# First attention: near distances as products over all features, far distances as products over 64 features a side in two halves of the rows

## Chip, core and metric

The kernel runs on one core of a Trainium2 chip. The metric is the device time of one execution in microseconds (us). TensorE (PE) multiplies, with its weight loads shown apart (PEld); VectorE (DVE), ScalarE (ACT) and GpSimd (POOL) work on rows; SyncE (SP) only issues DMAs. Each engine works through its own queue in order.

## The reference, cut to what matters

The network is an attention with relative positions, a mixture of experts, a second attention and the same mixture again, each added to its input. Only the first attention is changed. It has 4 batch rows of 1024 positions, 128 features, 8 heads:

```python
attn = einsum('bnqd,bnkd->bnqk', Q + rel_embed_bias, K)
positions = get_positional_embed(L, 192)      # (2 L - 1) x 192
rel_k = (positions @ w_rel_pos_k)             # for every distance and head
attn_pos = relative_shift(einsum('bnqd,nkd->bnqk', Q + rel_pos_bias, rel_k))
out = softmax(attn + attn_pos) @ V
```

The 192 features of a distance d are three kinds of 32 and the same 96 times the sign of d: exponentials of |d|, steps (1 where 2^n - 1 > |d|, for n = 1 to 32) and gamma densities of |d|. So on one side (d below 0, or d above 0) a sign is constant, and a step feature is constant between 2^n - 1 and the next power: from |d| = 127 to 1023 only the four steps n = 7 to 10 ever change.

## The kernel before

Work goes by blocks, one for each batch row and head (32 blocks), and each block by eight tiles of 128 query rows. Before the blocks, a setup loop over the heads turns and joins the weights (`turn_weights`, `join_weights`) and `distances` (L535) makes `relk`, the products of all 2048 distances' features with the head's joined weights: 128 x 2048 a head, kept in SBUF.

One loop over steps t (L706) writes out the order of the work by hand; its instructions stand on each engine in the order of the program:

- `relative(t + 5)` (L584): for tile i, the products of its 128 rows with a window of 1152 columns of `relk` (L594, 1024 columns into one PSUM buffer `rp`; L598, 128 columns into `rt`). ACT copies both into `xr` (L599, L600), and SP writes `xr` into a scratch tensor in DRAM (L603).
- `shift(t + 4)` (L606): SP reads the scratch back with rows one element shorter than they were written, which shifts each row by its number; this is `s`.
- `softmax(t)` (L614): content scores `sp` on PE (L622, 1024 columns), then one DVE instruction adds `s` and gives the row maximum (L627), then ACT takes the exponential and the row sum (L632).
- `transposed(t - 1)` (L635): DVE turns the probabilities in 32 x 32 squares into `at` (L641), and a reciprocal of the sum (L644).
- `values(m)` (L646), at the second step of the next block: 128 products of four row groups of 32 rows each (L655) into two PSUM buffers `op`; copies by ACT (L665) and DVE (L667) give `oT`. As `at` has one buffer, the first two tiles of a block are turned behind it, at its third step.
- `outputs` (L670), twice a block: four products `yp` (L674) and four DVE updates of the residual rows (L680).
- `make_keys` (L572), once a block: `kp` on PE (L576), copied by ACT to `kT` (L581).

PSUM has two pools here: `big` (three buffers of 1024 columns, for `rp`, `sp`, `op`, `kp`, taken in turn) and `small` (two buffers of 512 columns, for `rt`, `yp` and small products, taken in turn). They fill PSUM. A buffer is taken again when its last reader is done.

For three of the batch rows the routing of the experts (`dispatch`), and for each next batch row its layer norm (`rows`), run beside this loop in small steps.

One float32 product in the code is two records of PE in the trace.

Of the kernel before, what the change touches and what calls it, by code (L numbers as in the profile page):

```python
# [12 lines left out]
F32 = mybir.dt.float32  # L13
I32 = mybir.dt.int32
AF = mybir.ActivationFunctionType
ALU = mybir.AluOpType
AX = mybir.AxisListType

P = 128
B, L, D = 4, 1024, 128  # L20
NB = L // P
H = 8
R = 192
RW = 2 * L
WIN = L + P
E = 8
HID = 256
# [37 lines left out]
def block_kernel(ctx: ExitStack, tc: tile.TileContext, a: dict, out: bass.AP):  # L65
# [318 lines left out]
    with ExitStack() as sa:  # L384
# [6 lines left out]
        dram = sa.enter_context(  # L391
            tc.tile_pool(name="a_skew", bufs=8, space=bass.MemoryType.DRAM)
        )
        relk = [w1[:, :RW], w1[:, RW:], ring.rearrange("p a t d -> p (a t d)")]
        relk += [wp.tile([P, RW], F32, tag=f"relk{h}", name=f"relk{h}") for h in range(3, H)]

        joint = [wp.tile([P, 2, P], F32, tag=f"joint{h}", name=f"joint{h}") for h in range(H)]
        bo = wp.tile([P, D], F32, tag="a_bo", name="a_bo")
# [28 lines left out]
        with ExitStack() as s0:  # L427
# [39 lines left out]
            wr_views = (a["w_rel"][:R2, :], a["w_rel"][R2:, :])  # L467
            eb = wload("eb", [P, H], a["eb"], nc.gpsimd)
            rb = wload("rb", [P, H], a["rb"], nc.gpsimd)
            posf = {}  # L470
            for k in range(3):
                wq.load("wq", P, a["w_qs"], nc.sync, k)
                other = nc.scalar if k == 0 else nc.sync
                wk.load("wk", P, a["w_ks"], other, k)
                wr0.load("wr0", R2, wr_views[0], nc.sync, k)
                wr1.load("wr1", R2, wr_views[1], other, k)
                wv.load("wv", P, a["w_vs"], nc.sync, k)
                load_wo(other, k)
                if k == 0:
                    for c in (0, 2):  # L480
                        for half, eng in ((0, nc.sync), (1, nc.scalar if c == 0 else nc.sync)):
                            posf[half, c] = wload(
                                f"pos{half}_{c}", [R2, L],
                                a["pos"][half * R2 : (half + 1) * R2, c * 512 : (c + 2) * 512], eng,
                            )
            for b in range(B):
                nc.sync.dma_start(out=xs[b], in_=x_view[b])
                if b == 0:
                    nc.sync.dma_start(out=bo, in_=a["b_out"].to_broadcast([P, D]))
            turns, halves, scores = {}, {}, {}  # L490

            def turn_weights(h):
# [25 lines left out]
            def join_weights(h):  # L518
                wT, qe, qr, kk = turns.pop(h)
                jp = small(f"jp{h}")  # L520
                nc.tensor.matmul(jp[:, :P], kk, qe, start=True, stop=True)
                nc.tensor.matmul(
                    jp[:, P : 2 * P], wT[:, 2 * P : 3 * P], wo[h], start=True, stop=True
                )
                for k in range(2):
                    nc.tensor.matmul(
                        jp[:R2, (2 + k) * P : (3 + k) * P],
                        wT[:, 3 * P + k * R2 : 3 * P + (k + 1) * R2], qr, start=True, stop=True,
                    )
                nn = w0.tile([R2, 2 * P], F32, tag="nn", name=f"nn{h}", bufs=2)  # L530
                nc.scalar.copy(nn, jp[:R2, 2 * P :])
                nc.vector.tensor_copy(joint[h].rearrange("p k c -> p (k c)"), jp[:, : 2 * P])
                halves[h] = nn

            def distances(h, c):  # L535
                nn = halves[h]
                ps = big(f"rkps{h}_{c}")
                for half in range(2):
                    for k in range(2):
                        nc.tensor.matmul(  # L540
                            ps[:, k, :], nn[:, half * P : (half + 1) * P],
                            posf[half, c][:, k * 512 : (k + 1) * 512],
                            start=(half == 0), stop=(half == 1),
                        )
                out_rk = relk[h][:, c * 512 : (c + 2) * 512]
                if c == 0:
                    nc.scalar.copy(out_rk, ps.rearrange("p a c -> p (a c)"))
                else:
                    nc.vector.tensor_copy(out_rk, ps.rearrange("p a c -> p (a c)"))

            xn_a0 = w0.tile([P, NB, D], F32, tag="xn", name="xn_a0")
            first_rows = rows(0, xn_a0)
            with tc.manual_schedule():
                turn_weights(0)
                turn_weights(1)
                join_weights(0)
                for h in range(H):
                    distances(h, 0)
                    if h + 1 < H:
                        join_weights(h + 1)  # L560
                    distances(h, 2)
                    if h + 2 < H:
                        turn_weights(h + 2)
                    if 2 <= h <= 4:
                        next(first_rows, None)

        hp = sa.enter_context(tc.tile_pool(name="a_h", bufs=2))
        N = len(blocks) * NB
        AHEAD = 5
        keys, written, skewed, probs, rinvs, sums, turned_sums = {}, {}, {}, {}, {}, {}, {}  # L570

        def make_keys(m):  # L572
            b, h = blocks[m]
# [7 lines left out]
            nc.scalar.copy(kT, kp.rearrange("p a c -> p (a c)"))  # L581
            keys[m] = kT

        def relative(n):  # L584

            b, h = blocks[n // NB]
            i = n % NB
            rk = relk[h]
            lhsT = xTs[b][:, i * P : (i + 1) * P]
            base = (NB - 1 - i) * P  # L590
            xr = hp.tile([P, WIN], F32, tag="xr", name=f"xr{n}", bufs=3)
            rp = big(f"rp{n}")
            for c in range(2):
                nc.tensor.matmul(  # L594
                    rp[:, c, :], lhsT, rk[:, base + c * 512 : base + (c + 1) * 512], start=True, stop=True
                )
            tail = small(f"rt{n}")
            nc.tensor.matmul(tail[:, :P], lhsT, rk[:, base + L : base + WIN], start=True, stop=True)  # L598
            nc.scalar.copy(xr[:, :L], rp.rearrange("p a c -> p (a c)"))  # L599
            nc.scalar.copy(xr[:, L:WIN], tail[:, :P])  # L600

            scratch = dram.tile([P, WIN + 1], F32, tag="skew", name=f"skew{n}")
            nc.sync.dma_start(out=scratch[:, :WIN], in_=xr)  # L603
            written[n] = scratch

        def shift(n):  # L606

            scratch = written.pop(n)
            s = hp.tile([P, L], F32, tag="s", name=f"s{n}", bufs=7)
            shifted = bass.AP(scratch.tensor, scratch.offset + P, [[WIN, P], [1, L]])  # L610
            nc.sync.dma_start(out=s, in_=shifted)
            skewed[n] = s

        def softmax(n):  # L614

            b, h = blocks[n // NB]
            i = n % NB
            kT = keys[n // NB]
            s = skewed.pop(n)
            sp = big(f"sp{n}")  # L620
            for c in range(2):
                nc.tensor.matmul(  # L622
                    sp[:, c, :], xTs[b][:, i * P : (i + 1) * P], kT[:, c * 512 : (c + 1) * 512],
                    start=True, stop=True,
                )
            nmax = hp.tile([P, 1], F32, tag="nmax", name=f"nmax{n}", bufs=4)
            nc.vector.tensor_tensor_reduce(  # L627
                out=s, in0=sp.rearrange("p a c -> p (a c)"), in1=s, scale=-1.0, scalar=BIG,
                op0=ALU.add, op1=ALU.min, accum_out=nmax,
            )  # L630
            total = hp.tile([P, 1], F32, tag="total", name=f"total{n}", bufs=6)
            nc.scalar.activation(s, s, AF.Exp, bias=nmax, scale=-1.0, accum_out=total)  # L632
            probs[n] = (s, total)
# [36 lines left out]
        def outputs(m, oT, i0):  # L670
            b, h = blocks[m]
            yp = small(f"yp{m}_{i0}")
            for k in range(4):
                nc.tensor.matmul(  # L674
                    yp[:, k * P : (k + 1) * P], oT[:, i0 + k, :, :].rearrange("p g c -> p (g c)"),
                    joint[h][:, 1, :], start=True, stop=True,
                )
            for k in range(4):
                x_t = xs[b][:, i0 + k, :]
                nc.vector.scalar_tensor_tensor(  # L680
                    x_t, yp[:, k * P : (k + 1) * P], rinvs[m][:, i0 + k : i0 + k + 1], x_t,
                    ALU.mult, ALU.add,
                )
# [19 lines left out]
        coming = iter(())  # L703
        oT = None
        with tc.manual_schedule():
            for t in range(-AHEAD, N + 5):  # L706
                m, i = divmod(t - NB, NB)
                if t == -AHEAD:
                    make_keys(0)
                if 0 <= t + AHEAD < N:  # L710
                    relative(t + AHEAD)
                if 0 <= t + AHEAD - 1 < N:
                    shift(t + AHEAD - 1)
                if t == 4:
                    for w_t, view in late:
                        nc.gpsimd.dma_start(out=w_t, in_=view)
# [28 lines left out]
                    transposed(t - 1)  # L745
                if 1 <= m <= 3 and i in (2, 4, 6):
                    experts_weights(3 * (m - 1) + i // 2 - 1)
                if m >= 0 and i == 2:
                    outputs(m, oT, 0)
                if m >= 0 and i == 4:  # L750
                    outputs(m, oT, 4)
                    if m % H == H - 3:
                        next(coming, None)
# [540 lines left out]
```

## Time and profile before

| what | value |
|---|---|
| median of 23 runs | 2745.55 us |
| lowest and highest | 2740.62, 2756.26 us |
| the profiled execution: time | 2753.86 us |
| its span, first to last instruction | 2751.8 us |
| mean granted TensorE clock | 0.974 |
| first `values` starts | 136.4 us into the span |
| first attention ends (last `yp`) | 1615 us |
| one block of the first attention | 47.09 us, 24 of 31 of them within 1 us |

Durations below come from the one profiled execution, which was 8.3 us (0.3%) longer than the median. A duration in the trace is one instruction's record. ACT and DVE records overlap the next one's by up to 0.1 us, and PE's records include the time until a result has left the array, so that what an instruction holds its engine for is read from start to start. Idle time of an engine matters only where it is on the path that ends last.

### The profile page before, as it was taken

The page shows a single profiled execution, that of the slowest core. Times are in us where ns is not written, and L with a number is a line of the kernel's source. Part 1 is how long each engine was busy: PE and PEld are TensorE (multiplying, and loading weights), DVE is VectorE, ACT ScalarE, POOL GpSimd, SP SyncE. Part 2 cuts the span into 40 slices and gives each one's busy share as a digit, 9 for nine tenths or more (in the row PEclk, how much of TensorE's full clock was granted, in tenths as well). Part 3 has the DMA queues.
Part 4 walks back from the last instruction along what each step waited for, and adds up shares of the span by engine and source line. Part 5 has one row for each costly group of instructions (what it writes and reads, how often), then busy time and mean ns, then how long its engine had stood idle before and what let it go on. Part 6 is the DMA issues. An engine that isn't in the chain of part 4 may idle for free.

```text
span 2751.8 us, 47428 instructions
## 1 busy us (share of the span) xinstructions
PE 2675.0 (97%) x18928; PEld 1637.0 (59%) x18928; DVE 1407.1 (51%) x3278; ACT 1334.1 (48%) x2478; POOL 536.9 (20%) x691
## 2 busy tenths in 40 slices
PE   8999999999999999999999999999999999999895
PEld 4465656566565666666665666655555455554563
DVE  3345353545545454545445355466546466574454
ACT  2434353444444443544534345555566656556442
POOL 3121000000200001200002005543212215122275
PEclk9999999999999999999999999989999999999897
DMA  8777565755757565666657413300000001000143
GB/s 217 234 225 244 164 220 172 231 190 170 232 168 228 179 199 189 208 199 204 228 182 231 164 54 108 87 14 7 1 1 1 1 1 32 1 7 11 57 128 100
DMA packets 150955, 363.59 MB, mean 132 GB/s; under 512 B 16384, under 2 KB 74272, under 8 KB 150608
## 3 DMA queue, kind: packets, MB, share of 16 engines
q1 hardware_dynamic: 134832, 319.89, 36.0%
q0 software_dynamic: 15264, 39.92, 5.7%
q8 instruction: 150, 2.46, 0.4%
q10 hardware_dynamic: 640, 0.75, 0.1%
q14 instruction: 69, 0.57, 0.1%
HBM read 176.69 MB, written 183.76 MB: 131 GB/s over the span
## 4 chain that ended last, share of the span: by engine, by line
PE 92%; DVE 3%; DMA 2%; POOL 1%; issue 1%; ACT 1%; SPq 0%; ACTq 0%; POOLq 0%; DVEq 0%
PE op L655 16%; PE rp L594 16%; PE sp L622 15%; PE t_b L1079 9%; PE s_b L1022 9%; PE o_b L1100 5%; PE h_f L830 3%; PE h_g L830 3%; PE yp L674 2%; PE rt L598 2%; PE kp L576 2%; PE rkps L540 2%; PE yp_f L859 1%; PE qk_b L969 1%; PE yp_g L859 1%
## 5 line engine op out<-in xcount | busy, mean ns | idle before, releaser
L627 DVE CUSTOM_DVE_ANT_0 s<-sp,s 128x1024 f32<-128x1024 f32 x256 | 313.0, 1223 | 373.5 <-PE sp L622 373.2
L632 ACT ACTIVATE s<-s,nmax 128x1024 f32<-128x1024 f32 x256 | 294.1, 1149 | 413.9 <-DVE nmax L627 413.9
L622 PE MATMUL sp<-kT,xT 128*128 128x512 f32 x1024 | 484.4, 596 | 2.3 <-ACT kT L581 1.6
L655 PE MATMUL op<-at,xrep 32*128 32x256 f32 (+1 forms) x8448 | 455.8, 371 | 3.4 <-DVE nmax L627 3.1
L655 PEld LDWEIGHTS op<-at,xrep 32*128 32x128 f32 x8448 | 423.9, 187 | 47.0 <-issue 23.5
L1079 PE MATMUL t_b<-qm,ka_b 32*128 32x512 f32 x1152 | 424.4, 665 | 3.4 <-DVE m L1031 1.4
L1082 ACT ACTIVATE pt_b<-t_b 128x512 f32<-128x512 f32 x576 | 333.0, 615 | 160.0 <-PE t_b L1079 127.8
L1022 PE MATMUL s_b<-ka_b,qa_b 32*128 32x128 f32 (+3 forms) x2304 | 384.2, 408 | 1.6 <-DVE m L1031 1.3
L1031 DVE TENSOR_REDUCE m<-s_b 128x1 f32<-128x512 f32 (+3 forms) x480 | 287.1, 649 | 112.2 <-PE s_b L1022 87.4
L641 DVE STREAM_TRANSPOSE at<-s 128x1024 f32<-128x1024 f32 x256 | 315.8, 1238 | 0.2 <-ACT s L632 0.2
L594 PE MATMUL rp<-relk,xT 128*128 128x512 f32 x640 | 303.0, 596 | 0.0
L1022 PEld LDWEIGHTS s_b<-ka_b,qa_b 32*128 32x128 f32 x2304 | 227.1, 195 | 107.7 <-issue 41.7
L599 ACT COPY xr<-rp 128x1024 f32<-128x1024 f32 x256 | 256.3, 1001 | 71.0 <-issue 36.5
L622 PEld LDWEIGHTS sp<-kT,xT 128*128 128x128 f32 x1024 | 175.1, 191 | 128.0 <-issue 123.3
L667 DVE COPY oT<-op 128x256 f32<-128x256 f32 (+1 forms) x66 | 24.4, 411 | 398.7 <-PE op L655 398.7
L594 PEld LDWEIGHTS rp<-relk,xT 128*128 128x128 f32 x640 | 116.4, 190 | 127.1 <-issue 124.7
L665 ACT COPY oT<-op 128x256 f32<-128x256 f32 (+1 forms) x66 | 20.9, 369 | 351.9 <-PE op L655 351.9
L1079 PEld LDWEIGHTS t_b<-qm,ka_b 32*128 32x128 f32 x1152 | 149.0, 189 | 59.5 <-DVE m L1031 24.6
L170 POOL COPY beats<-beats 1x1 f32<-1x1 f32 x240 | 42.9, 179 | 602.5 <-DVE beats L167 601.7
L1100 PE MATMUL o_b<-pt_b,va_b 128*32 128x512 f32 x1152 | 146.2, 628 | 0.0
L594 PE MATMUL rp<-w,xT 128*128 128x512 f32 x256 | 121.2, 596 | 0.2 <-ACT xr L599 0.2
L598 PEld LDWEIGHTS rt<-relk,xT 128*128 128x128 f32 x320 | 60.8, 190 | 76.5 <-issue 75.3
(274 smaller groups left out, 3087.9 us busy)
## 6 DMA issues: line engine op xcount, KB each, us to landing
skew<-xr SPq DMA_DIRECT2D x256, 576.0 KB, 3.9
s<-skew SPq DMA_DIRECT2D x256, 512.0 KB, 4.5
ring<-sorted SPq DMA_DIRECT2D x40, 256.0 KB, 3.3
xrep<-stored POOLq DMA_DIRECT2D x16, 512.0 KB, 8.5
sorted<-joint POOLq DMA_DIRECT2D x4, 1472.0 KB, 18.4
res_f<-y_f SPq DMA_DIRECT2D x20, 256.0 KB, 2.5
res_g<-y_g SPq DMA_DIRECT2D x20, 256.0 KB, 2.4
w<-in_w POOLq DMA_DIRECT2D x16, 256.0 KB, 5.5
```

Of the source, the lines that this page charges most:

```text
L594: nc.tensor.matmul(rp[:, c, :], lhsT, rk[:, base + c * 512 : base + (c + 1) * 512], start=True, stop=True)
L599: nc.scalar.copy(xr[:, :L], rp.rearrange("p a c -> p (a c)"))
L622: nc.tensor.matmul(sp[:, c, :], xTs[b][:, i * P : (i + 1) * P], kT[:, c * 512 : (c + 1) * 512], start=True, stop=True,)
L627: nc.vector.tensor_tensor_reduce(out=s, in0=sp.rearrange("p a c -> p (a c)"), in1=s, scale=-1.0, scalar=BIG, op0=ALU.add, op1=ALU.min, acc ...
L632: nc.scalar.activation(s, s, AF.Exp, bias=nmax, scale=-1.0, accum_out=total)
L641: nc.vector.transpose(sums[m][:, i, :], s)
L655: nc.tensor.matmul(ops[g // 2][:, g % 2, :n], xrep[r, j, :], at[r, tiles, j * 32 : (j + 1) * 32], start=(j == 0), stop=(j == 31),)
L1022: nc.tensor.matmul(banks[m][:, q * w : (q + 1) * w], qa[r, k + q, tok], ka[r, k0 : k0 + w], start=True, stop=True,)
L1031: nc.vector.tensor_reduce(m2[:, 4 * g + k : 4 * g + k + nh, c], ps[:, : nh * w].rearrange("p (k c) -> p k c", c=w), AX.X, ALU.max,)
L1079: nc.tensor.matmul(ps, ka[rows[g], j * P : (j + 1) * P], qm[rows[g], :], start=True, stop=True)
L1082: nc.scalar.activation(pt[:, g, :], ps, AF.Exp, scale=HD ** -0.5)
L1100: nc.tensor.matmul(op[g * 32 : (g + 1) * 32, :], va[:, j, :], pt[:, g, :], start=(j == i), stop=(i == 0 or j == i - 1),)
```

## The change

The window of 1152 distances of a tile is cut in three. The 256 nearest are products over all 192 features, as before, from a table `near` of 256 columns a head (instead of 2048). For the distances from 128 on, on either side, the step features are taken out, and what is left are 64 features a side (32 exponentials, 32 gamma densities):

- `distances` makes, for every head, `near` (256 columns), eight columns of sums of step weights (`sums_of`, four ranges on each side), and `sides`, 128 x 128: joined weights of the 64 features of the negative side and of the positive one.
- `make_sides(m)`, once a block: `qf` = the rows' coefficients for those features, 128 x 1024, side 0 in partitions 0 to 63 and side 1 in 64 to 127.
- `relative` now works on a pair of tiles, at every second step, six tiles ahead. Two products of 264 columns (`near` and the eight sums), and the far distances of both tiles, whose two sides are products of 64 rows each, side 0 from one half of the partitions and side 1 from the other, into two `big` buffers, `far` 0 and `far` 1.
- DVE copies the eight sums into `xr`, ACT copies the 256 near columns, and ACT writes the far ones in pieces between the limits 127, 255, 511 and 1023, each with its sum of steps as a bias.
- The tiles of a block go in the order 0, 7, 1, 6, 2, 5, 3, 4, so that a pair has 896 far columns on each side. `shift` reads both tiles of a pair; `outputs` stands at steps 3 and 5 instead of 2 and 4 of a block; `s` has 9 buffers instead of 7, `xr` 4 instead of 3.
- In the setup only 256 columns of all the features and 896 of the far ones are loaded for each side, and the first batch row is loaded before the last weights.

```diff
+RANGES = ((7, 127), (8, 255), (9, 511), (10, 1023))
+NEAR = 2 * P
+FAR = L - P
...
-            def distances(h, c):
-                nn = halves[h]
-                ps = big(f"rkps{h}_{c}")
+            def distances(h):
+                nn, wT, qr = halves.pop(h)
+                ps = big(f"rkps{h}")
                 for half in range(2):
...
+                    nc.tensor.matmul(
+                        ps[:, 0, :NEAR], nn[:, half * P : (half + 1) * P], nearf[half],
+                        start=(half == 0), stop=(half == 1),
+                    )
+                nc.tensor.matmul(ps[:, 1, :R], qr, wT[:, 3 * P :], start=True, stop=True)
+                nT = w0.tile([P, R], F32, tag="nT", name=f"nT{h}", bufs=2)
+                nc.scalar.copy(nT, ps[:, 1, :R])
+                nc.scalar.copy(near[h][:, :NEAR], ps[:, 0, :NEAR])
...
+                for k, op in ((0, ALU.subtract), (1, ALU.add)):
+                    nc.vector.tensor_tensor(
+                        side[:, k, :, :], kinds[:, 0, 0::2, :], kinds[:, 1, 0::2, :], op
+                    )
+                    nc.vector.tensor_tensor(both[:, k, :], kinds[:, 0, 1, :], kinds[:, 1, 1, :], op)
+                sums_of = near[h][:, NEAR:].rearrange("p (s n) -> p s n", n=4)
+                for n in range(4):
+                    nc.vector.tensor_reduce(
+                        sums_of[:, :, n], both[:, :, RANGES[n][0] :], AX.X, ALU.add
+                    )
...
-        AHEAD = 5
+        AHEAD = 6
+        ORDER = [0, 7, 1, 6, 2, 5, 3, 4]
...
+        def make_sides(m):
+            b, h = blocks[m]
+            fps = big(f"fp{m}")
+            for c in range(2):
+                nc.tensor.matmul(
+                    fps[:, c, :], sides[h], xTs[b][:, c * 512 : (c + 1) * 512],
+                    start=True, stop=True,
+                )
+            qf = hp.tile([P, L], F32, tag="qf", name=f"qf{m}", bufs=2)
+            nc.scalar.copy(qf, fps.rearrange("p a c -> p (a c)"))
...
+        def relative(n):
...
+            pair = [ORDER[(n + k) % NB] for k in range(2)]
+            xr = [
+                hp.tile([P, WIN + 8], F32, tag="xr", name=f"xr{n + k}", bufs=4) for k in range(2)
+            ]
+            far = [big(f"far{n}_{side}").rearrange("p a c -> p (a c)") for side in range(2)]
...
+            for k in range(2):
+                ps = small(f"near{n + k}")
+                lhsT = xTs[b][:, pair[k] * P : (pair[k] + 1) * P]
+                nc.tensor.matmul(ps[:, : NEAR + 8], lhsT, near[h], start=True, stop=True)
+                x0 = P * pair[k]
+                nc.vector.tensor_copy(xr[k][:, WIN:], ps[:, NEAR : NEAR + 8])
+                nc.scalar.copy(xr[k][:, x0 : x0 + NEAR], ps[:, :NEAR])
+            for ones_of in itertools.zip_longest(*pieces):
+                for side, piece in enumerate(ones_of):
+                    if piece is not None:
+                        i, at, f0, w = piece
+                        r = slice(64 * side, 64 * (side + 1))
+                        nc.tensor.matmul(
+                            far[side][:, at : at + w], qf[r, i * P : (i + 1) * P],
+                            far_feats[r, f0 : f0 + w], start=True, stop=True,
+                        )
+            for k in range(2):
+                i = pair[k]
+                for side in range(2):
+                    for c, (_, d0) in enumerate(RANGES):
...
+                        if c0 < c1:
+                            col = WIN + 4 * side + c
+                            nc.scalar.activation(
+                                xr[k][:, c0:c1], far[side][:, src0 : src0 + c1 - c0], AF.Identity,
+                                bias=xr[k][:, col : col + 1],
+                            )
+                scratch = dram.tile([P, WIN + 1], F32, tag="skew", name=f"skew{n + k}")
+                nc.sync.dma_start(out=scratch[:, :WIN], in_=xr[k][:, :WIN])
...
-                if 0 <= t + AHEAD < N:
+                    make_sides(0)
+                if t % 2 == 0 and t + AHEAD < N:
                     relative(t + AHEAD)
-                if 0 <= t + AHEAD - 1 < N:
+                elif t % 2 and t + AHEAD - 1 < N:
                     shift(t + AHEAD - 1)
+                    shift(t + AHEAD)
+                if t % NB == NB - 1 and 1 <= t // NB + 2 < len(blocks):
+                    make_sides(t // NB + 2)
...
-                if m >= 0 and i == 2:
+                if m >= 0 and i == 3:
                     outputs(m, oT, 0)
-                if m >= 0 and i == 4:
+                if m >= 0 and i == 5:
                     outputs(m, oT, 4)
```

## Prediction

> **What bounds the kernel now.** I read the busy times and the chain first, then one block, then one tile of it.
>
> ```profile
> PE 2675.0 (97%) x18928; PEld 1637.0 (59%) x18928; DVE 1407.1 (51%) x3278; ACT 1334.1 (48%) x2478; POOL 536.9 (20%) x691
> ...
> PE 92%; DVE 3%; DMA 2%; POOL 1%; issue 1%; ACT 1%; SPq 0%; ACTq 0%; POOLq 0%; DVEq 0%
> ```
>
> TensorE is busy all the time and is 92% of the chain that ended last. By stretches (columns: us, PE, weight loads, DVE, ACT, POOL, granted clock, DMA share, GB/s), one block of the first attention:
>
> ```profile
> 183.50:230.60 47.10, 47.10 (x361) 29.52 (x360) 22.17 (x42) 20.45 (x35) 11.00 (x13) 1.00 0.74 230
> ```
>
> A block takes 47.09 us, all of it PE; ACT and DVE work 20 and 22 us. The groups of lines and one tile of the timeline (start, us) give the prices:
>
> ```profile
> L599 ACT COPY xr<-rp 128x1024 f32<-128x1024 f32 x256 | 256.3, 1001 | 71.0 <-issue 36.5 <-DMA skew<-xr 12.7 <-PE rp L594 11.7
> L600 ACT COPY xr<-rt 128x128 f32<-128x128 f32 x256 | 68.8, 269 | 0.0
> L970 ACT ACTIVATE qa_b<-qk_b,bbq 128x512 f32<-128x512 f32 x32 | 22.0, 687 | 32.7 <-PE qk_b L969 32.7
> ```
>
> ```profile
> 226.99 1.22 DVE L627 CUSTOM_DVE_ANT_0 s<-sp,s 128x1024 f32<-128x1024 f32 x1 [3.04 <-PE sp L622]
> ...
> 228.13 1.24 DVE L641 STREAM_TRANSPOSE at<-s 128x1024 f32<-128x1024 f32 x1
> 228.25 1.15 ACT L632 ACTIVATE s<-s,nmax 128x1024 f32<-128x1024 f32 x1 [2.09 <-DVE nmax L627]
> ...
> 229.40 0.99 ACT L599 COPY xr<-rp 128x1024 f32<-128x1024 f32 x1
> ...
> 230.29 0.27 ACT L600 COPY xr<-rt 128x128 f32<-128x128 f32 x1
> ```
>
> Start to start: an exp holds ACT for 1.15, a 1024-column copy for 0.89 (its record less 0.10). A softmax reduction holds DVE for 1.14 and its exp starts 1.26 after it. Transpose and reciprocal hold DVE for 1.20, the four updates of L680 for 1.02 (252.07 to 253.09). PE takes 1.72 for `sp`, `kp` (1024 columns, 1.68 ns each), 0.89 for the four `yp`, 14.12 for `op`; a reader starts 0.21 behind PE's slot, PE 0.05 behind ACT.
>
> **What the change takes from PE.** Per pair of tiles 2304 columns (3.87 us) go. In come two `near` of 264 (0.89) and 896 columns on each side, 1.50 if the two halves of the rows run at once, 3.01 if not. No row has two halves; the nearest is `op`: four groups of 32 rows, 256 records in 14.03, 0.055 each, where 256 columns alone take 0.215, so four run at once. I take 1.50. Changing between 128 rows and row groups: 0.1 before `op` (228.72 + 1.72 to 230.53) and up to 0.3 behind it; I take 0.1 and 0.2. `make_sides` adds 1.72 a block. PE's own work: 8 `sp` 13.76, `kp` and `fp` 3.44, `yp` 1.78, four pairs 4 x 2.69 = 10.76, `op` 14.12: 43.86, 3.2 less than 47.09.
>
> **What it puts on ACT.** The 1024-column copy becomes a near copy of 256 (0.275, as in the pair of L665: 0.65 - 0.375) and biased pieces. The built order has 8, 10, 10, 12 pieces in the four pairs, 1792 columns each. Price: L970, biased from PSUM: 687 - 100 = 0.59 for 512; at 0.817 ns a column (L600 to L599) that is 0.17 fixed. Bounds: 0.065 fixed (L600, no bias) and 0.28 (L109, two operands by pointer, 484 for 128 columns). I take 0.17, the same form: 2.82, 3.16, 3.16, 3.50 a pair, against 2.11 for the copies removed.
>
> The Trainium skill ("ScalarE: Activation LUTs", What ACT_TABLE_LOAD costs) gives a pointer operand about 93 ns and a biased ACTIVATE 280 ns + 0.833 ns a column, 93 of it overlapped. That makes my estimate by that page 0.187 fixed, some 0.7 us a block more than the row; L970's 687 is below its 707, so the row stands.
>
> **The new wait.** `big` has three PSUM buffers, taken in turn. A pair now takes two (`far` 0 and 1) and two `sp` two more, so the second `sp` sits in its own pair's `far` 0, and in the built order it waits for ACT. Behind it on PE stand `yp` and the next pair; behind those everything. ACT can't run the next pair early, as its queue has the second tile's exp first. Two more waits are in the built order: the near copy waits for DVE's copy of the eight bias columns (same bank), and with `small`'s two buffers the second `near` behind `outputs` waits for the four updates (L680) of the `yp` whose buffer it takes; those stand on DVE behind a reduction and a transpose. On SP the reads `s` stand behind both writes of their pair; at least five tiles (over 25 us) pass until they are needed, against 3.9 + 4.5 us landing, so I count nothing.
>
> **The loop.** R is when ACT has read the last of `far` 0. Four legs, from R to R:
> - Leg A (values inside): 0.05 + `sp` 1.72; `op` 14.12; two `near` 0.89; 0.1 + `far` 1.50; 0.21; 8 pieces 2.82 = 21.41.
> - Leg B: `sp` of leg A ended 1.1 before R, then DVE has that reduction and the two transposes held back by `op`: free at R + 2.64. Reduction 1.14, transpose 1.20, updates 1.02: 6.00. `near` 0.05 + 0.44, `far` 1.60, 0.21: 8.30. 8 pieces until `far` 0 is free, 2.72: 11.02.
> - Leg C: `sp` until 1.77, 0.21, reduction 1.14, transpose 1.20, updates 1.02: 5.34; `near`, `far`, 0.21: 7.64; 8 pieces 2.61: 10.25.
> - Leg D: `fp`, `sp`, `kp` 5.21, two `near` 0.89, `far` 1.60, 0.21: 7.90; 9 pieces 2.68: 10.58.
>
> Sum 53.26 a block, 6.17 more than now. PE idles 2.95 us in leg B (second `near`: 3.10 to 6.05), 2.29 in leg C, and about 1 us before each R. With the bounds of a piece (33 on the path) 49.8 to 56.9.
>
> **The clock.** Such gaps cost the clock (same columns):
>
> ```profile
> 1590.60:1594.10 3.50, 1.71 (x7) 0.49 (x5) 3.50 (x11) 1.32 (x3) 0.00 (x0) 0.99 0.00 0
> 1594.10:1597.50 3.40, 2.14 (x40) 2.14 (x44) 3.40 (x7) 1.45 (x4) 0.00 (x0) 0.50 0.01 2
> ...
> 1614.50:1617.90 3.40, 1.67 (x13) 1.19 (x12) 1.99 (x8) 1.16 (x2) 1.21 (x3) 1.00 0.43 105
> ...
> 2167.50:2170.90 3.40, 1.64 (x10) 1.07 (x10) 0.92 (x4) 2.35 (x7) 0.48 (x1) 1.00 0.00 0
> 2170.90:2174.30 3.40, 3.40 (x17) 2.90 (x20) 0.00 (x0) 1.51 (x5) 2.34 (x1) 0.50 0.00 0
> ```
>
> Stretches of 3.4 us in which PE idled 1.7 to 1.8 were twice followed by half clock for two stretches and more, once not. If it takes 2.05 idle in one stretch, a gap of 2.95 or 2.29 does it in (gap + 3.41 - 4.1) / 3.41 of all positions: 0.66 + 0.47 = 1.13 times a block. Each doubles a `near` and a `far` (1.95) and some of the `sp` behind (0.55): 2.5. So 2.8 a block; bounds 0 (no drop) and 5.0 (both gaps, each time).
>
> The Trainium skill ("TensorE: Matmul & The Clock Gate", Why this matters for your kernels) allows gaps up to about 3 us; by it the clock would stay and the 2.8 fall away. The row at 1590.6 has two gaps below 2 us and dropped, so I go by the row.
>
> **Around the loop.** Dispatch and row norms of other stages run in these queues: DVE has (94.76 - 4 x 22.17) + 4.7 + 1.6 = 12.3 us of it per batch row, ACT about 6; PE hid it. Half on the path: 9 a batch, 27 for three (0 to 54). The setup loses 49 of the 59 us of `rkps` (L540; 256 and 192 columns a head stay, 1.2 us), so that ACT (1.9 us a head) and DVE (2.6, eight small operations added) lead instead of PE's 8.3: 3.5 a head after the last weights, which land at about 25 us, and the first `kp` at about 42 instead of 84.6. From there to the first `op` it is 51.7 us now; then it is three pairs at 4.3, write and read of the first tile 3.9 + 4.5, some 3 to start, four legs without values or updates (8.5, 7.7, 7.7, 10.6) and 1.8: 59. Together -35 (-20 to -45, DMA being busy 0.92 there now).
>
> **Sum**, on the profiled execution (2753.86; its span 2751.8): the last interval between values has hardly any pairs (29.5 now) and stays; 30 x 6.17 = +185, +27, -35: 2931. With the clock, 30 x 2.8 = +84: 3015. The median of the runs is 8.3 lower: 2923 and 3007.
>
> **Rivals.**
> - The clock holds: 2923. For it: 1614.5. Chance 0.30; the forecast with drops, 3007, has 0.45.
> - Faster: the loop hides and PE stays the bound at 43.86 a block: 30 x -3.23 - 35 = 2622, median 2614. It decides from the point where ACT frees `far` 0 before the pair's first `sp` ends (1 us earlier in every leg) and the second `near` finds its buffer free (2 to 3 us earlier in legs B and C). For it: PE's 97%. Against: the built waits. 0.06.
> - The halves run one after the other: +1.50 in each leg, +180: 3103, with drops 3187. For it: no row of two halves. 0.11.
> - Pieces at a copy's price, no drops: 30 x -3.5: 2818. 0.06.
> - The legs lose what they save and the time is the same: 0.02.
>
> The range 2840 to 3110 leaves out the faster, same and cheap cases and about half of the fourth: 0.2. Bound for "no change" is 0.2% (5.5 us), what this kernel's runs can tell.
>
> **What would show it.** Right: values 53 to 56 us apart; PE's idle time led by ACT before the second `sp` and by DVE before `near`; half clock inside the stage; ACT and DVE each under 70% busy; `far` of a pair in 1.5 us. Wrong: blocks at 44 us with PE full, or ACT full without gaps.

## The result, and the profile after

The changed kernel takes 3035.49 us, the median of 8 runs (3029.27 to 3041.71), against 2746.31 us before: a ratio of 1.1055 (95% interval 1.1039 to 1.1072), slower by a tenth. Its profiled execution takes 3045.68 us, its span 3043.9.

The busy times and the chain of waits, to lay beside those of before:

```profile
PE 2687.8 (88%) x19232; PEld 1626.7 (53%) x19232; DVE 1437.2 (47%) x3590; ACT 1556.4 (51%) x3542; POOL 536.8 (18%) x691
...
PE 73%; DVE 12%; ACT 7%; issue 5%; DMA 2%; POOL 1%; SPq 0%; DVEq 0%; POOLq 0%; ACTq 0%
```

TensorE went from 97% of a shorter span to 88% of a longer one: the time is in its gaps. DVE and ACT, 3% and 1% of the chain before, are 12% and 7%. What TensorE waited for (us in total, times, longest):

```profile
PE near L653 <- DVE x L763: 185.7, 57, 4.9
PE sp L705 <- ACT xr L680: 51.7, 62, 4.4
```

These are the two waits that the prediction read from the built order. One leg B, its engines side by side (start, us; at the end the idle time ahead and what ended it):

```profile
489.19 1.24 DVE L724 STREAM_TRANSPOSE at<-s 128x1024 f32<-128x1024 f32 x1
...
490.40 1.22 DVE L724 STREAM_TRANSPOSE at<-s 128x1024 f32<-128x1024 f32 x1
490.45 0.61 PE L653 MATMUL near<-near,xT 128*128 128x264 f32 x2
...
491.59 1.20 DVE L710 CUSTOM_DVE_ANT_0 s<-sp,s 128x1024 f32<-128x1024 f32 x1
492.72 1.24 DVE L724 STREAM_TRANSPOSE at<-s 128x1024 f32<-128x1024 f32 x1
...
493.92 1.10 DVE L763 SCALAR_TENSOR_TENSOR x<-yp,rinv,x 128x128 f32<-128x128 f32 x4
...
495.08 1.25 PE L653 MATMUL near<-near,xT 128*128 128x264 f32 x2 [4.02 <-DVE x L763]
496.25 3.36 PE L662 MATMUL far<-far_feats,qf 64*128 64x512 f32 x12
...
502.40 1.98 PE L705 MATMUL sp<-kT,xT 128*128 128x512 f32 x4 [0.49 <-ACT xr L680]
```

The second `near` waits 4.02 us, while VectorE works off, without a gap, the rest of a transpose, a reduction, another transpose and the four updates. The `near` and `far` behind it then run at half clock: `far` takes 3.36 us, where the next pair's takes 1.78.

Over the whole span the time went like this. From the first value product (`op`) to the 31st, 30 blocks, it is 1729.95 us against 1427.14: +302.8. The first `op` comes at 129.51 in place of 136.36: -6.9. All the rest: -3.8. The sum is the 292.1 by which the span grew.

### The profile page after: what moved, and what is told of

It reads as the page before. It is cut to its first block, busy times and chain, and to the rows that moved or that the text cites. A ratio compares the mean times of both kernels' runs of the same rounds, so it can differ in the third digit from the quotient of the medians.

```text
span 3043.9 us, 49858 instructions
## 1 busy us (share of the span) xinstructions
PE 2687.8 (88%) x19232; PEld 1626.7 (53%) x19232; DVE 1437.2 (47%) x3590; ACT 1556.4 (51%) x3542; POOL 536.8 (18%) x691
## 4 chain that ended last, share of the span: by engine, by line
PE 73%; DVE 12%; ACT 7%; issue 5%; DMA 2%; POOL 1%; SPq 0%; DVEq 0%; POOLq 0%; ACTq 0%
PE op L738 15%; PE sp L705 9%; PE far L662 9%; PE t_b L1166 8%; PE s_b L1109 7%; ACT xr L680 6%; PE o_b L1187 4%; DVE at L724 4%; PE near L653 4%; PE h_f L917 3%; PE h_g L917 2%; DVE x L763 2%; DVE s L710 2%; PE fp L617 2%; DMA skew<-xr 2%
## 5 line engine op out<-in xcount | busy, mean ns | idle before, releaser
L705 PE MATMUL sp<-kT,xT 128*128 128x512 f32 x1024 | 516.3, 633 | 51.7 <-ACT xr L680 51.7
L680 ACT ACTIVATE xr<-far,xr 128x256 f32<-128x256 f32 (+11 forms) x1280 | 398.5, 435 | 168.5 <-PE far L662 168.4
L705 PEld LDWEIGHTS sp<-kT,xT 128*128 128x128 f32 x1024 | 187.8, 200 | 318.9 <-issue 200.4
L653 PE MATMUL near<-near,xT 128*128 128x264 f32 x512 | 173.3, 444 | 198.8 <-DVE x L763 185.7
L662 PE MATMUL far<-far_feats,qf 64*128 64x512 f32 (+3 forms) x1280 | 290.0, 590 | 1.5 <-ACT xr L680 1.3
L653 PEld LDWEIGHTS near<-near,xT 128*128 128x128 f32 x512 | 91.4, 206 | 256.4 <-DVE x L763 209.4
L662 PEld LDWEIGHTS far<-far_feats,qf 64*128 64x128 f32 x1280 | 138.0, 235 | 144.4 <-issue 115.4
L656 ACT COPY xr<-near 128x256 f32<-128x256 f32 x256 | 91.2, 374 | 133.0 <-issue 67.0
## 6 DMA issues: line engine op xcount, KB each, us to landing
sorted<-joint POOLq DMA_DIRECT2D x4, 1472.0 KB, 17.2
```

Of the source, the lines that this page charges most:

```text
L653: nc.tensor.matmul(ps[:, : NEAR + 8], lhsT, near[h], start=True, stop=True)
L662: nc.tensor.matmul(far[side][:, at : at + w], qf[r, i * P : (i + 1) * P], far_feats[r, f0 : f0 + w], start=True, stop=True,)
L680: nc.scalar.activation(xr[k][:, c0:c1], far[side][:, src0 : src0 + c1 - c0], AF.Identity, bias=xr[k][:, col : col + 1],)
L705: nc.tensor.matmul(sp[:, c, :], xTs[b][:, i * P : (i + 1) * P], kT[:, c * 512 : (c + 1) * 512], start=True, stop=True,)
```

## The experiments

Times are ratios to the kernel before on the same chip, with 95% intervals. The block is the mean of the 30 intervals from `op` to `op` in the profile; half clock is the time in them at 0.50, a block; the idle time is TensorE's in all 30.

| kernel | ratio | block, us | half clock, us a block | TensorE idle, us |
|---|---|---|---|---|
| before | 1 | 47.57 | 0 | 1.6 |
| changed | 1.1055 (1.1039 to 1.1072) | 57.66 | 7.4 | 254 |
| `again`: changed, another chip | 1.1021 (1.0976 to 1.1067) | 57.56 | 6.8 | 256 |
| `e1_fill` | 1.0798 (1.0766 to 1.0830) | 55.19 | 0.3 | 136 |
| `e2_near` | 1.0997 (1.0957 to 1.1038) | 57.01 | 5.8 | 253 |
| `e3_nosteps` | 1.1010 (1.0968 to 1.1051) | 57.52 | 10.2 | 241 |
| `e4_split` | 1.0970 (1.0921 to 1.1020) | 56.56 | 7.4 | 236 |
| `e5_early` | 1.0367 (1.0334 to 1.0400) | 51.34 | 1.4 | 145 |
| `e6_early_split` | 1.0249 (1.0212 to 1.0287) | 50.36 | 1.9 | 108 |
| `e7_setup` | 1.1006 (1.0969 to 1.1042) | 57.44 | 6.6 | 256 |
| `e8_early24` | 1.0531 (1.0488 to 1.0573) | 52.63 | 4.0 | 158 |
| `e9_early24_sides` | 1.0359 (1.0321 to 1.0397) | 51.08 | 2.6 | 134 |
| `e10_both2_sides` | 1.0115 (1.0091 to 1.0139) | 49.12 | 0 | 105 |
| `e11_turns` | 0.9876 (0.9854 to 0.9898) | 47.00 | 0 | 46 |

The changed kernel itself, once more, on another chip:

> The changed kernel as it is, beside the others of this call, so that they are compared on one chip. Every theory: 1.1055 times the kernel before, within its interval (1.104 to 1.107).

1.1021 is a little below what was expected, but the two intervals overlap: between these two chips the ratio carries over to within 0.4%.

**Does the half clock cost anything?** `e1_fill` keeps every wait and gives TensorE more to do in its two long gaps:

```diff
-nc.tensor.matmul(ps[:, : NEAR + 8], lhsT, near[h], start=True, stop=True)
+again = {2: 6, 4: 4}.get(n % NB, 0) if k == 0 and n >= NB else 0
+for _ in range(1 + again):
+    nc.tensor.matmul(ps[:, : NEAR + 8], lhsT, near[h], start=True, stop=True)
```

> The first `near` product of a pair is done seven times over in leg B and five times in leg C, so that TensorE works (6 x 0.44 = 2.7 us and 4 x 0.44 = 1.8 us more) while the second `near` waits for the four updates; every result and every wait stays. Theory (the idle gaps bring the half clock, and the half clock costs about 2.5 us a block): most of the 51 half-clock stretches go, blocks from 57.7 to about 55.1 us, 55 to 90 us less than the changed kernel, about 2955 us, although TensorE has 4.4 us a block more to do. Rival (the half clock falls where TensorE waits anyway, the chain through ScalarE and VectorE sets the block): within 10 us of the changed kernel. Second rival (the added products delay what stands behind them): slower, up to 130 us.

The ratio fell by 0.0257 against the changed kernel and by 0.0223 against `again`, some 61 to 71 us, though TensorE had 4.4 us a block more to do, and half clock nearly vanished from the stage (7.4 to 0.3 us a block). The block fell by 2.4 to 2.5 us. The rival that the drops are free is out. What is left, 55.2, is the loop at nearly full clock. Its leg B, TensorE:

```profile
478.36 3.28 PE L655 MATMUL near<-near,xT 128*128 128x264 f32 x14
482.99 0.71 PE L655 MATMUL near<-near,xT 128*128 128x264 f32 x2 [1.35 <-DVE x L765]
```

The gap is 1.35 in place of 4.02, and the `near` behind it takes 0.71, not 1.25.

**Is it the wait for the updates?** `e2_near` moves the `near` products of legs B and C one step earlier, ahead of the `yp`:

```diff
 def relative(n):
-    ... near products and their copies ...
+    if n not in nears: near_part(n)
+    xr = nears.pop(n)
...
     make_keys(t // NB + 1)
+if t % NB in FIRST and t + 1 + AHEAD < N:      # FIRST = (3, 5)
+    near_part(t + 1 + AHEAD)
```

> The two `near` products of a pair, with their copies, are issued one step earlier for the pairs of legs B and C, ahead of the `yp` products, so that the second `near` finds a buffer of `small` free and no longer waits for the updates of L763; all else stays. Theory (that wait is what legs B and C are made of, and its gaps bring the half clock): gaps ahead of `near` go, leg B from 14.6 (11.0 at full clock) to about 8.3 us, leg C from 10.6 to about 8, blocks of 47.5 to 51 us, about 2740 to 2840 us. Rival (the chain is ScalarE's pieces and the wait for `far` 0, and the wait for the updates lies beside it): blocks stay above 55 us, 2960 us or more.

The theory's number failed: 1.0997, inside the interval of `again`. The rival's number came out, but not by its cause, ScalarE's pieces. The wait for the updates is gone from the list, and another has its size (first line: the waits of the whole span; then the same place of the timeline):

```profile
PE yp L768 <- ACT xr L640: 179.3, 60, 4.7
```

```profile
496.98 1.20 DVE L721 CUSTOM_DVE_ANT_0 s<-sp,s 128x1024 f32<-128x1024 f32 x1
...
498.23 1.15 ACT L726 ACTIVATE s<-s,nmax 128x1024 f32<-128x1024 f32 x1 [2.28 <-DVE nmax L721]
...
499.38 0.63 ACT L640 COPY xr<-near 128x256 f32<-128x256 f32 x2
499.78 2.07 PE L768 MATMUL yp<-joint,oT 128*128 128x128 f32 x8 [3.77 <-ACT xr L640]
```

Now `yp` waits for a buffer of `small`: the `near` copy that frees it stands on ACT behind the exp, the exp behind VectorE's second reduction. The edit changed the last link and left the reduction in the loop. It does not show that the updates cost nothing.

**Is it ScalarE's pieces?** `e3_nosteps` leaves the biases out and copies the far columns on ScalarE in fewer and larger copies; `e4_split` gives half of the pieces to VectorE:

```diff
 # e3_nosteps
-for c, (_, d0) in enumerate(RANGES): ... nc.scalar.activation(..., bias=...)
+c0, c1 = (0, i * P) if side == 0 else (i * P + NEAR, WIN)
+nc.scalar.copy(xr[k][:, c0:c1], far[side][:, place[side, k] : place[side, k] + c1 - c0])
 # e4_split
+if side == 0: ... nc.scalar.activation(...) as before
+else: nc.vector.tensor_scalar(xr[k][:, c0:c1], far[side][...], xr[k][:, col : col + 1], None, ALU.add)
```

> The steps are left out: each tile's far columns are copied without biases, one copy a tile and side (2 in pair 0/7, 4 in the others, in place of 8, 10, 10, 12 pieces); the scores are then without the coarse step features. By the rows a pair's copies take 1.6 to 1.7 us of ScalarE in place of 2.8 to 3.4, 5.7 us a block less. Theory (the pieces stand on the path in every leg): blocks shorter by 4 to 5.5 us, 120 to 165 us less than the changed kernel. Rival (VectorE's updates set legs B and C, the pieces are hidden there): 0 to 60 us less.

> The pieces of side 1 (half of them) go to VectorE in place of ScalarE, so that the two `far` buffers are read at once. Theory (the wait for ScalarE's pieces is on the path in every leg): `far` 0 is free 1.2 to 1.5 us earlier in each leg, blocks shorter by 3 to 5 us, 90 to 150 us less than the changed kernel. Rival (VectorE, whose reduction, transpose and updates make up legs B and C, is the chain and now has 6 us a block more in its queue): no change or slower, up to 100 us.

Neither moved the time clearly: 1.1010 lies inside the interval of `again`, and 1.0970 just below it, with an interval that overlaps. In `e3_nosteps` the copies take

```profile
L671 ACT COPY xr<-far 128x896 f32<-128x896 f32 (+6 forms) x448 | 231.6, 599 | 185.2 <-PE far L662 184.2
```

against 398.5 us for the changed kernel's 1280 pieces, and the wait of `sp` for `far` 0 falls from 51.7 to 9.3 us; but the wait of `near` for the updates grows from 185.7 to 195.2 us, `op` now waits 21.8 us for ScalarE's exps, and half clock grows from 7.4 to 10.2 us a block. VectorE's rows in leg C show why. The changed kernel:

```profile
501.95 1.23 DVE L710 CUSTOM_DVE_ANT_0 s<-sp,s 128x1024 f32<-128x1024 f32 x1 [5.42 <-PE sp L705]
503.10 1.24 DVE L724 STREAM_TRANSPOSE at<-s 128x1024 f32<-128x1024 f32 x1
...
504.42 1.22 DVE L710 CUSTOM_DVE_ANT_0 s<-sp,s 128x1024 f32<-128x1024 f32 x1
505.57 1.24 DVE L724 STREAM_TRANSPOSE at<-s 128x1024 f32<-128x1024 f32 x1
...
506.78 1.10 DVE L763 SCALAR_TENSOR_TENSOR x<-yp,rinv,x 128x128 f32<-128x128 f32 x4
```

From the first reduction to the end of the updates it is 5.93 us, with hardly any gap. The second reduction needs the second `sp`, which waits for the pieces, but it also stands behind the first transpose. In `e3_nosteps` the same five run from 500.15 to 505.94: the pieces were some 1.4 us shorter, and VectorE's row only 0.14. Two chains of nearly one length end together, and to cut one alone shows little. The half clock hid part of what was saved too: at the rate of `e1_fill` (2.4 us for 7.1 us of half clock) the 2.8 us more cost 1 us a block, by estimate.

**VectorE's order.** `e5_early` issues `yp`, and so the updates, ahead of the `sp` of the same step; `e6_early_split` adds the split of `e4_split`.

```diff
+if m >= 0 and i in (3, 5):
+    outputs(m, oT, 0 if i == 3 else 4)
 if 0 <= t < N:
     softmax(t)
...
-if m >= 0 and i == 3:
-    outputs(m, oT, 0)
-if m >= 0 and i == 5:
-    outputs(m, oT, 4)
```

> The `yp` products with their updates are issued ahead of the same step's `sp`, not behind it; nothing else moves. VectorE's updates then stand ahead of that step's reduction and the transpose behind it, and the next pair's second `near` finds its buffer free. Theory (legs B and C are a loop of VectorE's queue, `sp`, reduction, transpose, updates, `near`, and any order that leaves the exp or the reduction inside that loop stays as long): leg B becomes 0.05 + `sp` 1.72 + two `near` 0.89 + `far` 1.60 + 0.21 + pieces 2.72 = 7.2 us, up to 7.9 where the near copies stand behind the second exp; leg C the same; with A 20.6 and D 10.7 blocks of 46.4 to 47.5 us, and with fewer half-clock stretches 46.4 to 49.5 in the run: 250 to 340 us less than the changed kernel, a ratio to the kernel before of 0.985 to 1.02. Rival (as with `near` one step earlier, another link of the same length takes over): ratio above 1.08.

> The early `yp` products as in the run before, and the pieces of side 1 on VectorE. Theory (with the updates out of the loop, what sets a leg is ScalarE's pieces and the wait for `far` 0; halved, they free it 1.2 to 1.5 us earlier, and TensorE's own 43.9 us become the bound): blocks of 44 to 46.5 us, ratio 0.955 to 0.99. Rival (VectorE becomes the chain once its queue holds 6.5 us more a block): ratio at or above that of the early products alone.

1.0367: 6.2 us a block and most of the half clock went with two moved calls, where moving `near` or lightening the pieces had shown no clear gain. The block is 51.3, not the 46.4 to 49.5 of the theory, since the updates still stand behind two transposes in leg B:

```profile
PE near L653 <- DVE x L763: 60.4, 38, 2.6
PE fp L617 <- ACT xr L680: 37.9, 26, 2.4
PE sp L705 <- ACT xr L680: 36.3, 50, 1.3
```

The split now brings 0.0118 (32 us), where without the early `yp` it brought no clear gain: what the pieces cost can be seen once the updates are out of the loop. Neither run reached the expected ratio.

**Setup.** `e7_setup` issues `turn_weights(h + 2)` ahead of `join_weights(h + 1)` and `distances(h)`.

> Setup alone: the transposes of head h + 2 are issued ahead of `join_weights(h + 1)` and `distances(h)`, not behind them, so that VectorE makes the next head's factors ahead of its eight small operations of this head. Theory (the setup's missing gain is a chain of latencies from head to head, with waits for `kk` of 5.1, 2.1, 2.1 and 1.8 us): the first `kp` comes 8 to 11 us earlier than at 60.1 us, and the whole is 6 to 11 us shorter, a ratio lower by 0.002 to 0.004. Rival (the write and read of the first tiles, with DMA busy, set the first values whatever comes before): within 2 us of the changed kernel.

In the profile the waits of `jp` for `kk` from 25 us on (11.1 us in all in the changed kernel) are one wait of 4.3 for another tile, the first `kp` comes at 51.05 in place of 59.07 (in `again`) and the first `op` at 121.90 in place of 126.63. So 8 us went ahead of `kp`, and 4.7 are left at `op`. The time, 4.7 us below that of `again`, is less than the 6 to 11 of the theory, and the two intervals overlap: as a time the gain is not shown.

**Toward a version that beats both.** `e8_early24` puts the two groups of `yp` at steps 2 and 4, `e9_early24_sides` also orders the pieces by side, then by tile, so that `far` 0 is read after half of them; `e10_both2_sides` puts both groups at step 2 and takes in the setup order; `e11_turns` moves transposes.

```diff
 # e9_early24_sides
-for k in range(2):
-    for side in range(2):   # the pieces of one tile, then the other
+for side in range(2):
+    for k in range(2):
 # e10_both2_sides, ahead of softmax(t)
+if m >= 0 and i == 2:
+    outputs(m, oT, 0)
+    outputs(m, oT, 4)
 # e11_turns, ahead of softmax(t); behind it, turn_to(t - 2) at i in (2, 4, 6)
+if m >= 0 and i in (0, 4, 6):
+    turn_to(t - 1 if i == 0 else t - 3)
```

> The `yp` products and their updates are issued two steps of the order earlier than in the changed kernel's places: for tiles 0 to 3 ahead of the `sp` of step 2, for tiles 4 to 7 ahead of that of step 4 (the run with the early products had steps 3 and 5, where the updates stood behind two transposes: its trace still has 60 us of waits of `near` for the updates). Theory: those 60 us go; a leg is the loop `sp` 1.77, reduction, exp 4.4, near copies 4.95, eight of ten pieces 7.65; blocks of 47 to 48.5 us, a ratio of 0.99 to 1.015. Rival (the waits for `far` 0 grow by what the waits for the updates lose): the ratio stays within 0.01 of 1.0367.

> As the run before, and ScalarE's pieces go by side first, then by tile: `far` 0 has been read after half of a pair's pieces (1.4 to 1.7 us) in place of all but the last two (2.5 to 2.7). Theory (`far` 0 is the last link): legs B and C at 6.8 us of TensorE's own work, blocks of 45 to 46.5 us, a ratio of 0.955 to 0.985, faster than the kernel before. Rival (VectorE's reductions and transposes, or the exp ahead of the near copies on ScalarE, are the link that ends last): within 0.006 of the run before.

> Both groups of `yp` products and their updates ahead of the `sp` of step 2, ScalarE's pieces by side first, and the setup order of the run on the setup. In the run before, the second group, at step 4, waited 2.2 us a block for a `near` copy to leave its buffer (73.5 us in all); at step 2 both buffers of `small` are free. Theory: that wait goes, legs B and C are `sp` 1.77 + 0.21 + reduction 1.14 + transpose 1.20 + bias copies 0.23 + near copies 0.65 + half of the pieces 1.6 = 6.8 us, leg A 21.9, D 9.6 to 10.7: blocks of 45.3 to 48 us, and 5 us less from the setup: a ratio of 0.95 to 0.995, faster than the kernel before. Rival (the yp products in one place only move the wait of legs B and C to the next buffer of `big`, and TensorE's own work with its changes between 128 rows and halves is above 47 us): a ratio of 1.005 to 1.03.

> As the run before, with VectorE's transposes moved: each block's last three stand ahead of the reduction of the next block's tile 0, so that `op` no longer waits for the last of them (15.0 us in all); only one of the next block's, not two, stands between the reductions of tiles 2 and 3; the others stand behind the bias copies of steps 4 and 6, not ahead of them, and the `near` copies come 0.2 us earlier. Nothing else moves. Theory (VectorE's order in legs B to D holds the last links: 31.8 us of waits of `sp` for the reductions, 35.5 for the pieces, 15.0 of `op`): 0.65 us a block from `op`, 1.2 from leg B, up to 0.4 from C and D: blocks of 46.5 to 47.6 us, a ratio of 0.985 to 1.0. Rival (the links are ScalarE's exps and pieces): only `op`'s wait goes, a ratio of 1.003 to 1.008.

`e8_early24` missed both its theory and its rival: 1.0531, worse than with steps 3 and 5, as the second `yp` took a buffer that a `near` of its own step had just filled (`PE yp L757 <- ACT xr L656`, 73.5 us), whose copy stands behind VectorE again. The order by sides took off 0.0172, which is more than its rival allowed, but 1.0359 is far from its theory's 0.955 to 0.985: the wait of 73.5 us stayed. With both `yp` at step 2 no half clock is left in the stage; the ratio, 1.0115, still missed the theory and lies in the rival's range, and its waits named the next links:

```profile
PE sp L706 <- ACT xr L680: 35.5, 25, 1.7
PE sp L706 <- DVE nmax L711: 31.8, 37, 1.8
PE op L739 <- DVE rinv L728: 15.0, 24, 0.7
```

The transposes were moved to where VectorE is idle, and all but the first line nearly went: 0.9876, 2717.48 us (2710.87 to 2718.41), as expected. A plain block of `e11_turns` (columns: us, PE, weight loads, DVE, ACT, POOL, granted clock, DMA share, GB/s):

```profile
443.19:489.17 45.98, 45.10 (x369) 28.15 (x368) 23.30 (x52) 26.51 (x69) 3.15 (x4) 1.00 0.71 205
```

45.98 against the 47.10 of before, 45.10 of it TensorE's work at full clock. With the same products as the changed kernel, only issued in another order, the change is faster than before, by 1.2%. The stage gives only half of that: of the 35.6 us by which the span is shorter, 17.2 come from the 30 blocks, and 16.0 from the first `op`, at 120.39 in place of 136.36.

## Why the prediction was right, and where it was not

- **The sign and the blocks.** Predicted +185 for the legs and +27 for other stages' work, with +84 for the clock: 296 for 30 blocks. Measured: 302.8. That the sum is so near is in part luck. In `e1_fill`, at nearly full clock, the plain blocks take 54.38 us, 7.29 more than before: 219 us in 30 blocks for the legs, 10 for the blocks that carry other stages' work, and the 74 that are left for the clock. The prediction had the legs 34 too short, and the two other terms 17 and 10 too long. The middle block of the changed kernel, 57.4, lies above the 53 to 56 that were to be the sign.
- **The two waits** were read rightly out of the order, and are the first two in the list. `far` of a pair has records of 1.77 and 1.78 at full clock, 1.70 from start to next start, so the halves do run at once; that rival is out.
- **TensorE's own work** is 45.10 in the plain block of `e11_turns`, not 43.86. Most of the difference is `sp`: its eight take 14.78, not 13.76, from start to next start, the ends of records that stand ahead of a wait counted in. The `near` and `far` of four pairs take 10.87, not 10.76. The rival that TensorE stays the bound would so have had 2 us a block to win, not 3.2; it needed the two waits to go, and both stood.
- **The clock.** 47 drops in 30 blocks (1.6 a block against 1.13), 7.4 us of half clock a block, worth 2.4 to 2.5 by `e1_fill`, against 2.8. The 2.05 us of idle time in a stretch, from which the 1.13 were worked out, stand in no row; in the changed kernel drops came from 1.80 on (last section). So there were more drops than forecast, and each cost less, 1.6 us and not 2.5. The rival that the clock holds, to which I gave 0.30, is out.
- **What leg B is made of.** In the timeline shown, the second `sp` of leg A did not wait: it took the buffer that was released first, `far` 1, and leg A ended 0.9 earlier than the sum. Leg B lost that time again, and more: with R at the start of this `sp` (487.84), VectorE's first reduction starts 0.2 behind R, not 0.9 ahead of it, and the updates end at R + 7.1 (494.94), not 6.0. At nearly full clock, in a plain block of `e1_fill`, legs A to D take 20.55, 12.45, 10.65 and 10.73, against 21.41, 11.02, 10.25 and 10.58. Leg B is the mis-sized one; with the half clock of the timeline shown it took 14.6.
- **The pieces** were put on the path in every leg, and their bounds alone were given as 49.8 to 56.9 a block. `e3_nosteps` shows that the low end could not be reached that way: without the biases, at a copy's price, the block stays at 57.5, and would be some 54 without its half clock, by the same estimate as above. VectorE's chain of reduction, transpose, reduction, transpose, updates, at hand in the same built order, is as long. The step that failed is that the bounds were made on one chain and not on the next longest. A piece itself cost what was priced: 8, 10 and 12 in 2.81, 3.11 and 3.42 us.
- **The setup** is the mis-sized term that nothing made good: -35 predicted, -6.9 measured. On the profiled execution, 3045.7 against the 3015 of the sum, it makes 28 of the 31 us that the sum lacks; the errors of the blocks cancel to 7, and all the rest takes 4 off. From head to head (start of `jp`) it took 5.9 to 7.7 us, not 3.5, and once 12.9, where the layer norm of the first batch row stands between. I had priced the engines' work and left out the latencies: `jp` waits 17.0 us in all for `kk`, which VectorE makes behind its work for the head before. The clock was put at nothing there, too. From the start to the first `kp`, before and changed (columns as in the row of `e11_turns`):

```profile
0.00:84.60 84.60, 73.32 (x240) 39.00 (x241) 24.41 (x73) 21.29 (x42) 22.18 (x36) 1.00 0.75 184
0.00:60.10 60.10, 37.13 (x160) 31.21 (x161) 24.71 (x122) 17.55 (x48) 22.17 (x36) 0.80 0.93 242
```

TensorE has gaps there now, and 23.9 of these 60 us were at half clock. The first `kp` came at 60.1, not 42, and 69.4 us passed to the first `op`, not 59 (the terms listed for it add up to 60.6). `e7_setup` recovers 8 of the 18 us ahead of `kp`, with 17.1 us still at half clock; no run tells apart what the latencies and what the clock cost. What sets the 10 us behind `kp` stays open as well: the chain of waits gives 30% of the first 135 us to the writes of the first tiles, whose buffers `xr` are awaited; between 60 and 130 us a write lands after 6.9 us in the median, and 3.9 had been priced. A larger pool of `xr` wasn't tried.

## What to carry to other kernels

A change that shortens the bound engine's work by 2 us a block lost 10, because two short PSUM pools tied that engine to the ends of two other engines' queues: before a product is given a buffer, list what stands in the queues ahead of whoever frees it. Removing one link of such a loop tells little if the next is as long, as three runs here show; the cure was the order in which the off-path engines get their work, not less work. And gaps on TensorE are to be judged by what they do to its clock as well as by their length.

## What was not expected of the hardware

The clock is granted in stretches of 3.41 us (every drop in the stage of the changed kernel lasts 3.41 or 6.83), and what decides is how much of one stretch TensorE is idle. Around the gap of leg B in the changed kernel (same columns):

```profile
490.12:493.53 3.41, 0.94 (x7) 0.53 (x5) 3.41 (x7) 1.13 (x3) 0.00 (x0) 1.00 0.81 250
493.53:496.94 3.41, 1.86 (x4) 1.01 (x6) 1.73 (x8) 1.25 (x4) 0.00 (x0) 0.50 0.59 199
496.94:500.36 3.42, 3.42 (x13) 1.86 (x10) 0.00 (x0) 0.75 (x5) 0.00 (x0) 0.50 0.01 2
500.36:503.77 3.41, 2.92 (x7) 1.06 (x6) 1.82 (x3) 2.95 (x9) 0.00 (x0) 1.00 0.48 193
503.77:507.18 3.41, 1.96 (x12) 1.27 (x10) 3.37 (x8) 1.93 (x4) 0.00 (x0) 1.00 0.86 267
507.18:510.60 3.42, 2.66 (x15) 1.51 (x16) 0.94 (x5) 0.95 (x3) 0.00 (x0) 1.00 0.63 198
```

2.47 us idle in the first stretch is followed by half clock; the next, with 1.55 idle, does not bring the clock back, a full stretch of work does; 1.45 idle in the stretch before the last is followed by full clock. In the stage of the changed kernel each of the 47 drops followed a stretch with at least 1.80 us idle, and none with over 1.92 went without; in `e5_early` stretches with 1.68 to 1.98 went both ways. So in these traces it is about half a stretch, and a gap of 2.2 us can do it or not, by where the boundary falls. The Trainium skill ("TensorE: Matmul & The Clock Gate", Why this matters for your kernels) allows gaps up to about 3 us. The gap above is longer, but in the stage of `e5_early` none is over 2.6 us, and there are 11 drops, seven of them behind a single gap of 1.68, as here:

```profile
401.20:404.61 3.41, 1.73 (x7) 0.76 (x7) 3.41 (x9) 0.10 (x2) 0.00 (x0) 1.00 0.81 250
404.61:408.02 3.41, 3.41 (x14) 1.96 (x11) 1.27 (x4) 2.85 (x8) 0.00 (x0) 0.50 0.48 157
```

They do not agree, and the measurement decides.

VectorE takes the biased pieces from PSUM at ScalarE's price: five in 1.65 us beside five in 1.61 (`e4_split`).
